# A graph-attention kernel whose order is planned: other costs in the plan, and a dot product carried in the query rows

## The chip, the cores and the metric

The kernel runs on one core of a Trainium2 chip. The metric is the device time of one execution in microseconds (us), taken as the median of several executions. TensorE is PE in the profile (its weight loads are PEld), VectorE is DVE, ScalarE is ACT, GpSimd is POOL and SyncE, which only starts DMAs here, is SP.

## The reference

There are 32 batches of 512 nodes with 512 features, in float32, and one sparse 512 x 512 adjacency matrix `adj` (about 4 edges for each node). Two layers follow each other, both on a layer norm and a relu of their input:

```
h = relu(layernorm(x))
q, k, v = h @ Wq + bq, h @ Wk + bk, h @ Wv + bv        # 8 heads of 64
out = softmax(q k' / 8, over the edges of adj) v
x = x + out @ Wo + bo                                  # layer 0
h = relu(layernorm(x)) ; hw = h @ W
s1, s2 = hw @ a1, hw @ a2
att = softmax(leaky_relu(s1_i + s2_j) * adj, over all j)
x = x + elu(att @ hw + beta * hw)                      # layer 1
```

In layer 1 a pair without an edge has the exponent 0, so each row is a sum over all nodes plus a correction over its edges.

## The kernel before

**Tiles and stages.** A batch is 4 tiles of 128 nodes (T = 4). `stage_a(b)` fetches x, normalizes it, transposes it and makes queries (`queries`), keys and values (`keys_and_values`, with seven half products for each pair of tiles). They go to tables in DRAM: `qtab` for q, `tab` for k and v. `stage_b(b)` works through edges. Each tile of 128 nodes has 4 groups of 128 edge slots. For each group POOL gathers the rows of k and v of the edge's source (`gather`, L939) and the row of q of the edge's node (L959) by indirect DMA. `layer0` multiplies q and k (L990), sums each head (L993), takes the exponent on ACT (L999), weights the rows of v (L1004), and PE sums the edges of each node into PSUM (`edge_sums`, L977). The result is divided by the sum of the weights (L1028), transposed (L734), copied out of PSUM (L1041), multiplied by Wo (L41) and added to x (L1043). Then come the norm, the relu and two dot products with rows of W a (L1051): s2 as column 0 of the row `hx`, which is stored for layer 1, and s1 of the node in a tile of its own.

Layer 1 of batch b runs with layer 0 of batch b + 2 (LAG = 2), so that one gather brings k and v of one batch and hx of the older one in a single row of `tab`. The last two batches have no such partner, and gather hx alone from `th`. `edge_weights` adds s1 of the edge's node and s2 of its source (L1109), and makes the weights `wv`; `layer1` sums hx by them, adds the column sums of the whole batch (`cs`), and ends with the product by W (L41), the elu (L1171, L1172, L1176, L1177) and the write to the output.

**s1 for each edge.** Before the change, `self_sums` does this once in a batch: PE transposes the four columns of s1 (L1080), ACT copies them out, SP writes them to DRAM as one row (L1083) and reads that row back into all 128 partitions (L1088, 256 KB, into a buffer of the ring "q"). DVE multiplies it with the one-hot matrix OH (L1092) and sums groups of 32 (L1093), which leaves s1 of each edge's node in `s1e`. `self_sums` also makes the column sums: PE sums the rows of hx (L1071), with each of the 4 sums repeated in 32 rows, ACT copies them (L1075), PE transposes them, and DVE reduces all 512 columns of the result (L1077).

**What sets the order.** Nothing is issued in the order of the source. Each step is recorded by `op` with an engine, a cost in us, a key (the time at which it is wished, in steps S of 20 us for each tile) and what it reads and writes. `Plan.order` then plays the work through: on each engine it takes, of the steps that could start first, the one with the smallest `rank`, gives it a buffer of its ring, and books its cost. The instructions are issued in the order of the planned starts, and each engine keeps to that order on the chip. Three constants matter here. `PACE` (L71) multiplies the costs of DVE and ACT. `FREE` (L69) is subtracted from the key of those DVE and ACT steps that read or write PSUM, so that they come earlier. The rings (L271 on) give the number of buffers: a step that takes a buffer can't be planned before one of its ring is free, and on the chip it waits until the last reader of that buffer, a store included, is done.

The lines of the change as the profile names them: L787 (q out of PSUM), L859 (k and v out of PSUM), L890 (stores of q, k and v by SP), L959 (gather of q), L990, L993, L1075 to L1100 (`self_sums`), L1109 (s1 + s2).

Of the kernel before, what the change touches and what calls it, by code (L numbers as in the profile page):

```python
# [9 lines left out]
F32 = mybir.dt.float32  # L10
I32 = mybir.dt.int32
AF = mybir.ActivationFunctionType
ALU = mybir.AluOpType
# [18 lines left out]
KO, VO, HO = 0, 512, 512 + 8 * VW  # L32
HW_ = 520
ROW = HO + HW_
LAG = 2
DUMMY = 4

# [26 lines left out]
class Plan:  # L64
# [1 line left out]


    STAY, WAIT = 1.0, 0.2
    FREE = 5.0  # L69

    PACE = {"DVE": 0.9, "ACT": 0.93}  # L71

    LAG = {"PE": 0.25, "DVE": 0.12, "ACT": 0.2, "POOL": 0.15, "SP": 0.0}

# [4 lines left out]
    def buf(self, tag, name=""):  # L79
        return Buf(tag, name)  # L80
# [137 lines left out]
def kernel(  # L218
# [49 lines left out]
    def ring(n, shape, name):  # L268
        return [wtile(shape, f"{name}{i}") for i in range(n)]
# [4 lines left out]
        "S": ring(3, [P, C // 2, P], "S"),  # L274
        "oT": ring(1, [P, C, P], "oT"),
        "gT": ring(1, [P, C, P], "gT"),
        "q": ring(2, [P, D], "q"),
        "k": ring(2, [P, D], "k"),
        "v": ring(5, [P, H, VW], "v"),
        "kv": ring(5, [P, 2, ROW], "kv"),  # L280
        "qe": ring(2, [P, 2, D], "qe"),
        "w": ring(4, [P, D], "w"),
        "x1": ring(4 * LAG + 1, [P, D], "x1"),
        "hx": ring(4, [P, HW_], "hx"),
# [6 lines left out]
        "st": ring(3, [P, 6], "st"),  # L291
        "rd": ring(2, [P, T, H], "rd"),
        "dn": ring(3, [P, 3, T], "dn"),
        "s1": ring(2, [P, T], "s1"),
        "cs": ring(LAG + 1, [P, C], "cs"),
        "row": [dram.tile([N], F32, name=f"row{i}", tag=f"row{i}") for i in range(2)],
        "tab": [dram.tile([N + DUMMY, ROW], F32, name=f"tab{i}", tag=f"tab{i}") for i in range(LAG + 2)],
        "tkv": [dram.tile([N + DUMMY, HO], F32, name=f"tkv{i}", tag=f"tkv{i}") for i in range(LAG)],
        "th": [dram.tile([N + DUMMY, HW_], F32, name=f"th{i}", tag=f"th{i}") for i in range(LAG)],
        "qtab": [dram.tile([N + 1, D], F32, name=f"qtab{i}", tag=f"qtab{i}") for i in range(3)],  # L300
# [27 lines left out]
    def setup():  # L328
        nc.gpsimd.iota(OH.bitcast(I32), pattern=[[1, D]], base=1, channel_multiplier=0)
        nc.gpsimd.iota(idx[:, 0, 0:1], pattern=[[1, 1]], base=0, channel_multiplier=1)  # L330
        make_identity(nc, ident)
        nc.gpsimd.memset(mhalf, -0.5)
        nc.vector.memset(rings["qe"][-1], 0.0)
        nc.vector.memset(one32, 1.0 / G)
        for b in rings["hx"]:
            nc.vector.memset(b[:, D:], 0.0)
        for b in rings["v"]:
            nc.vector.memset(b[:, :, HD:], 0.0)
        for b in [rmax, dmax, fin]:
            nc.vector.memset(b, 0.0)  # L340

    def constants():

        def load(fn, dma=4096, w=()):
            op("SP", 0.1, 20.0, fn, w=w, dma=dma)

        for dst, src in ((bk_r, bk), (bq_r, bq)):
            load(lambda dst=dst, src=src: nc.sync.dma_start(dst, bcast_rows(src, D)), P * D * 4, [C_["rows"]])
        load(lambda: nc.sync.dma_start(beta_b, bcast_rows(beta, 1)))
        zero = rings["qe"][-1].rearrange("p a b -> p (a b)")  # L350
        for tag, n in (("tkv", D), ("qtab", D), ("th", HW_), ("tab", ROW)):
# [575 lines left out]
    def stage_b(b):  # L927
# [16 lines left out]
        for t in range(T):  # L944
            kb = base(T * b + t)
            slots = [buf("kv", f"kv{b}_{t}_{i}") for i in range(2)]
            held = [{n: buf(None, n) for n in ("K", "V", "H")} for _ in range(2)]
            of = {KO: "KVH", VO: "VH", HO: "H"}
            for g in range(NG):
                for tab, c0, c1 in st[b]["tab"]:  # L950
                    op("POOL", 1.3, kb - 0.85 * S + 0.1 * g, lambda sl=slots[g // 2], g=g, t=t, tab=tab, c0=c0, c1=c1: gather(
                        sl.ap[:, g % 2, c0:c1], tab, t, g),
                       r=[tab, C_["idx"]],
                       w=[(slots[g // 2], (g % 2, c0)), *((held[g // 2][n], (g % 2, "row")) for n in of[c0])],
                       dma=P * (c1 - c0) * 4)
            if s is not None:
                qs = [buf("qe", f"qe{b}_{t}_{i}") for i in range(2)]
                for g in range(NG):
                    op("POOL", 1.3, kb - 0.84 * S + 0.1 * g, lambda q=qs[g // 2], g=g, t=t: nc.gpsimd.indirect_dma_start(  # L959
                        q.ap[:, g % 2, :], None, s["qtab"].ap,  # L960
                        bass.IndirectOffsetOnAxis(ap=qidx[:, t, g : g + 1], axis=0),
                        bounds_check=N, oob_is_err=False),
                       r=[s["qtab"], C_["qidx"]], w=[(qs[g // 2], g % 2)], dma=P * D * 4)
            wvb = edge_weights(b - LAG, t, kb, slots, held) if old is not None else None
# [17 lines left out]
    def layer0(b, t, kb, slots, held, qs, weights):  # L982

        s = st[b]
        for i in range(2):
# [1 line left out]
            sb = buf("s", "s")  # L987

            def mult(qe=qe, sl=sl):
                nc.vector.tensor_tensor(qe.ap, qe.ap, sl.ap[:, :, KO : KO + D], op=ALU.mult)  # L990

            def total(qe=qe, sb=sb):
                nc.vector.tensor_reduce(  # L993
                    sb.ap, qe.ap.rearrange("p n (h f) -> p n h f", f=HD), axis=AX.X, op=ALU.add
                )

            def expo(sl=sl, sb=sb):
# [8 lines left out]
            op("DVE", 1.24, key, mult, r=use([sl], [held[i]], "K"), w=[qe])  # L1006
            op("DVE", 1.2, key, total, r=[qe], w=[sb])
# [55 lines left out]
    def self_sums(b, key):  # L1063
# [5 lines left out]
        def col_sums():  # L1069
# [10 lines left out]
        o = op("PE", 0.15, key + 0.485 * S, lambda: nc.tensor.transpose(ps.ap[0:T, 0:P], s["s1"].ap, ident), r=[s["s1"]], w=[ps])  # L1080
        plan.reserve(o, s1t)
# [3 lines left out]
        s1b, s1e = buf("q", f"s1b{b}"), buf("s1e", f"s1e{b}")  # L1085
        s["s1e"] = s1e

        op("SP", 0.1, key, lambda: nc.sync.dma_start(s1b.ap, row.ap.unsqueeze(0).to_broadcast([P, N])),  # L1088
           r=[row], w=[s1b], dma=P * N * 4)

        def pick():
            nc.vector.tensor_tensor(s1b.ap, OH, s1b.ap, op=ALU.mult)  # L1092
            nc.vector.tensor_reduce(  # L1093
                s1e.ap.rearrange("p t g -> p (t g)"), s1b.ap.rearrange("p (s r) -> p s r", r=G), axis=AX.X, op=ALU.add
            )

        op("DVE", 1.4, key + 0.8 * S, pick, r=[C_["OH"]], w=[s1b, s1e])
        op("DVE", 0.2, key + 0.9 * S, lambda: nc.vector.scalar_tensor_tensor(
            fin, s["mv1"].ap[:, :, 0:2], 0.0, fin, op0=ALU.mult, op1=ALU.add), r=[s["mv1"]], w=[C_["fin"]])
        op("DVE", 0.2, key + 0.9 * S, lambda: nc.vector.tensor_tensor(rmax, rmax, s["rd"].ap, op=ALU.max),  # L1100
           r=[s["rd"]], w=[C_["rmax"]])

    def edge_weights(b, t, kb, slots, held):

        s = st[b]
        k1 = kb + 0.6 * S
        z, wvb = buf("z", f"z{b}_{t}"), buf("wv", f"wv{b}_{t}")
        for i in range(2):
            op("DVE", 0.2, k1, lambda i=i: nc.vector.tensor_tensor(  # L1109
                z.ap[:, 2 * i : 2 * i + 2], s["s1e"].ap[:, t, 2 * i : 2 * i + 2], slots[i].ap[:, :, HO], op=ALU.add),  # L1110
               r=[s["s1e"], *use([slots[i]], [held[i]], "H")], w=[z])
# [318 lines left out]
```

## Time and profile before

| | |
|---|---|
| median of 10 runs | 2746.71 us (2740.95 to 2752.78) |
| the profiled execution | 2743.47 us |
| its span, first to last instruction | 2741.6 us |
| granted TensorE clock, mean | 0.989 |
| DMA | 796.71 MB, mean 291 GB/s |
| DMA queue of POOL (gathers) | 643.93 MB, 69.6% of 16 engines |
| DMA queue of SP (stores, loads) | 150.15 MB, 14.9% of 16 engines |

Times are of one profiled execution. Busy time of an engine counts its instructions, and "(x53)" behind it is their number. A line of the timeline gives the start, the duration, the engine, the line of the kernel, the operation, output and input, how many records were merged, and in brackets the idle time before it and what ended that. A float32 product is two records, so "x8" is four products. The granted clock is 1.00 where TensorE ran at full speed.

Queries, keys and values are made from the first microseconds on until 2553 us, and layer 0 of the first batch reaches its edges at 99 us. So the run has a fill at its start, a long middle that repeats every 82 us (one batch), and a drain from 2553 us on.

### The profile page before, as it was taken

To read this page: it belongs to the slowest core of one execution; us is meant where nothing else is said; L and a number is where in the kernel's file an instruction comes from. 1 tells how busy PE (TensorE), PEld (TensorE's weight loads), DVE (VectorE), ACT (ScalarE), POOL (GpSimd) and SP (SyncE) were. 2 spreads that over 40 slices of the span, in tenths; PEclk is the share of its full clock that TensorE was granted. 3 is DMA by queue.
4 is the path that set the end of the run, shared out by engine and by line. 5 is a ranking of instruction groups with operands and counts; after the bars stand their busy time and mean duration, and the time that the engine had idled before them with its cause. 6 is when DMAs were issued, how large, how long until landed. Compare 5 with 4: busy or idle time off the path is not lost.

```text
span 2741.6 us, 39873 instructions
## 1 busy us (share of the span) xinstructions
PE 2661.2 (97%) x10250; PEld 1210.8 (44%) x10250; DVE 2091.0 (76%) x5138; ACT 1936.6 (71%) x6245; POOL 1823.8 (67%) x1710
## 2 busy tenths in 40 slices
PE   8999999999999999999999999999999999999886
PEld 4444444444444444444444444444444444444332
DVE  8768778777777777787877777777778777777663
ACT  1557777777777677777777777777777777777763
POOL 2866676676676676776676676666666676676663
PEclk9999999999999999999999999999999999999988
DMA  5988898888898888988888888888898898898863
GB/s 178 295 260 324 316 307 294 311 293 304 304 306 290 304 305 279 328 295 292 310 302 297 306 301 302 299 306 301 296 314 304 282 319 289 296 321 281 300 208 106
DMA packets 242019, 796.71 MB, mean 291 GB/s; under 512 B 35267, under 2 KB 35395, under 8 KB 241782
## 3 DMA queue, kind: packets, MB, share of 16 engines
q0 software_dynamic: 156736, 643.93, 69.6%
q1 hardware_dynamic: 85046, 150.15, 14.9%
q8 instruction: 83, 1.36, 0.2%
q14 instruction: 154, 1.26, 0.1%
HBM read 624.70 MB, written 169.26 MB: 290 GB/s over the span
## 4 chain that ended last, share of the span: by engine, by line
PE 87%; DVE 4%; DMA 3%; ACT 3%; issue 2%; POOL 1%; another core or an unknown queue 0%; POOLq 0%; SPq 0%; DVEq 0%; ACTq 0%
PE pd L41 44%; PE pd L851 26%; PE pd L734 6%; PE pd L977 4%; PE px L977 4%; ACT kv L1004 2%; DMA kv<-tab,idx 2%; PE pd L911 1%; DMA qe<-qtab,qidx 1%; PE pd L1071 1%; DVE s L993 1%; DVE qe L990 0%; POOL kv L939 0%; DVE w L1028 0%; DMA x<-in_x_dram,perm 0%
## 5 line engine op out<-in xcount | busy, mean ns | idle before, releaser
L1004 ACT ACTIVATE kv<-kv 128x64 f32<-128x64 f32 x4096 | 1011.5, 336 | 5.6
L959 POOL DMA_INDIRECT qe<-qtab,qidx x512 | 557.8, 1089 | 264.6 <-issue 119.6
L939 POOL DMA_INDIRECT kv<-tab,idx x480 | 516.0, 1075 | 164.9 <-issue 111.1
L41 PE MATMUL pd<-w,gT 128*128 128x512 f32 x1024 | 467.3, 599 | 5.9 <-ACT gT L1162 4.9
L41 PE MATMUL pd<-wo,oT 128*128 128x512 f32 x1032 | 469.2, 598 | 1.6 <-ACT oT L1041 1.4
L41 PE MATMUL pd<-wq,hT 128*128 128x512 f32 x1024 | 462.8, 595 | 0.0
L759 POOL DMA_INDIRECT x<-in_x_dram,perm x252 | 355.1, 1409 | 89.7 <-issue 60.8
L990 DVE TENSOR_TENSOR qe<-qe,kv 128x1024 f32<-128x1024 f32 x256 | 313.0, 1223 | 41.6 <-DMA kv<-tab,idx 25.4
L993 DVE TENSOR_REDUCE s<-qe 128x16 f32<-128x1024 f32 x256 | 311.0, 1215 | 0.7
L41 PEld LDWEIGHTS pd<-w,gT 128*128 128x128 f32 x1024 | 196.2, 192 | 252.6 <-issue 234.6
L41 PEld LDWEIGHTS pd<-wo,oT 128*128 128x128 f32 x1032 | 196.6, 192 | 245.2 <-issue 232.6
L41 PEld LDWEIGHTS pd<-wq,hT 128*128 128x128 f32 x1024 | 194.5, 191 | 244.7 <-issue 241.9
L764 POOL DMA_INDIRECT out_dram<-w,perm x128 | 149.0, 1164 | 202.4 <-DVE w L1177 142.5
L746 POOL TENSOR_TENSOR mv<-mv,mhalf 128x1 f32<-128x1 f32 x256 | 166.5, 658 | 140.4 <-DVE mv L743 104.0
L851 PE MATMUL pd<-wk,hT 128*128 128x512 f32 x496 | 240.6, 610 | 4.9 <-ACT kv L999 2.4
L851 PE MATMUL pd<-wt,S 128*128 128x512 f32 x496 | 237.9, 602 | 1.9 <-ACT v L873 1.4
L851 PE MATMUL pd<-wv,S 128*128 128x512 f32 x496 | 233.5, 593 | 0.0
L734 PE MATMUL pd<-ident,w 128*128 128x128 f32 x1152 | 160.7, 278 | 30.8 <-DVE w L1028 15.6
L1051 DVE CUSTOM_DVE_ANT_0 w<-hx,wa_r 128x512 f32<-128x512 f32 x256 | 175.9, 687 | 9.1 <-ACT hx L753 6.3
L1171 ACT ACTIVATE w<-pd,dn 128x512 f32<-128x512 f32 x128 | 86.7, 677 | 135.8 <-PE pd L41 120.5
L1043 DVE TENSOR_TENSOR x<-pd,x 128x512 f32<-128x512 f32 x128 | 88.1, 689 | 122.8 <-PE pd L41 95.8
L741 DVE BATCH_NORM_STATS2 st<-x 128x6 f32<-128x512 f32 x256 | 176.4, 689 | 5.9 <-DMA x<-in_x_dram 1.7
(201 smaller groups left out, 3557.8 us busy)
## 6 DMA issues: line engine op xcount, KB each, us to landing
qtab<-q SPq DMA_DIRECT2D x124, 256.0 KB
tab<-hx SPq DMA_DIRECT2D x120, 260.0 KB
tab<-v SPq DMA_DIRECT2D x120, 260.0 KB
tab<-k SPq DMA_DIRECT2D x120, 256.0 KB
qe<-qtab,qidx POOLq DMA_INDIRECT x512
q<-row SPq DMA_DIRECT2D x32, 256.0 KB
kv<-tab,idx POOLq DMA_INDIRECT x480
x<-in_x_dram,perm POOLq DMA_INDIRECT x252
```

The costliest lines, as they stand in the source:

```text
L41: nc.tensor.matmul(out, lhsT, rhs, start=start, stop=stop)
L734: nc.tensor.transpose(p[:, ts(c, P)], src[:, ts(c, P)], ident)
L741: nc.vector.bn_stats(s6.ap, src.ap)
L759: nc.gpsimd.indirect_dma_start(dst, None, rows, bass.IndirectOffsetOnAxis(ap=perm[:, t : t + 1], axis=0), **lim)
L851: nc.tensor.matmul(p.ap, lhs()[:, c, :], rhs[:, c, :], start=first and c == 0, stop=c == K2 - 1, skip_group_check=True)
L939: nc.gpsimd.indirect_dma_start(dst, None, tab.ap, bass.IndirectOffsetOnAxis(ap=idx[:, t, g : g + 1], axis=0), bounds_check=N + DUMMY - 1, ...
L959: op("POOL", 1.3, kb - 0.84 * S + 0.1 * g, lambda q=qs[g // 2], g=g, t=t: nc.gpsimd.indirect_dma_start(q.ap[:, g % 2, :], None, s["qtab"]. ...
L977: nc.tensor.matmul(out(g), lhs(g), slots[g // 2].ap[:, g % 2, c0 : c0 + n], start=True, stop=True)
L990: nc.vector.tensor_tensor(qe.ap, qe.ap, sl.ap[:, :, KO : KO + D], op=ALU.mult)
L993: nc.vector.tensor_reduce(sb.ap, qe.ap.rearrange("p n (h f) -> p n h f", f=HD), axis=AX.X, op=ALU.add)
L1004: nc.scalar.activation(p[:, h, 0:HD], p[:, h, 0:HD], AF.Copy, scale=p[:, h, HD : HD + 1])
L1051: nc.vector.tensor_tensor_reduce(scr.ap, hx.ap[:, 1 : D + 1], row, 1.0, 0.0, op0=ALU.mult, op1=ALU.add, accum_out=dst)
```

## The change

- In the plan, `PACE` goes from 0.9 (DVE) and 0.93 (ACT) to 1.0, and `FREE` from 5 to 10, half a step.
- A row of q gets 4 more columns (QW = 516 in place of 512), and column 512 holds s1 of the same node two batches earlier, which DVE copies there. `qtab`, its stores and the gathers of q carry it. `edge_weights` adds s1 from the gathered q row (a buffer `qe`) in place of `s1e`.
- The way of s1 over transpose, row, broadcast and pick moves into `spread_s1`, and is left for the last two batches only.
- The ring "k" has one buffer in place of two, and "s1" three in place of two.
- The column sums: ACT scales them by 32 as it copies them, and DVE reduces every 32nd column only.

```
-    FREE = 5.0
+    FREE = 10.0
-    PACE = {"DVE": 0.9, "ACT": 0.93}
+    PACE = {"DVE": 1.0, "ACT": 1.0}
...
-        "q": ring(2, [P, D], "q"),
-        "k": ring(2, [P, D], "k"),
+        "q": ring(2, [P, QW], "q"),
+        "k": ring(1, [P, D], "k"),
-        "qe": ring(2, [P, 2, D], "qe"),
+        "qe": ring(2, [P, 2, QW], "qe"),
-        "s1": ring(2, [P, T], "s1"),
+        "s1": ring(3, [P, T], "s1"),
...
-        op("DVE", 0.7, key, lambda: nc.vector.tensor_tensor(q.ap, p.ap, bq_r, op=ALU.add), r=[p, C_["rows"]], w=[q])
+        op("DVE", 0.7, key, lambda: nc.vector.tensor_tensor(q.ap[:, 0:D], p.ap, bq_r, op=ALU.add), r=[p, C_["rows"]], w=[(q, "q")])
+        if b >= LAG:
+            s1 = st[b - LAG]["s1"]
+            op("DVE", 0.1, key, lambda: nc.vector.tensor_copy(q.ap[:, D : D + 1], s1.ap[:, t : t + 1]),
+               r=[(s1, t)], w=[(q, "s1")])
...
-        op("ACT", 0.6, key, lambda: nc.scalar.copy(csr.ap, pc.ap), r=[pc], w=[csr])
+        op("ACT", 0.6, key, lambda: nc.scalar.activation(csr.ap, pc.ap, AF.Copy, scale=float(G)), r=[pc], w=[csr])
...
-        op("DVE", 0.69, key + 0.5 * S, lambda: nc.vector.tensor_reduce(
-            cs.ap, pt.ap.rearrange("p (c q) -> p c q", c=C), axis=AX.X, op=ALU.add), r=[pt], w=[cs])
+        op("DVE", 0.2, key + 0.5 * S, lambda: nc.vector.tensor_reduce(
+            cs.ap, pt.ap[:, 0 :: G].rearrange("p (c q) -> p c q", c=C), axis=AX.X, op=ALU.add), r=[pt], w=[cs])
+        if b + LAG >= B:
+            spread_s1(b, key)
...
+            def add(i=i):
+                s1 = s["s1e"].ap[:, t, 2 * i : 2 * i + 2] if qs is None else qs[i].ap[:, :, D]
+                nc.vector.tensor_tensor(z.ap[:, 2 * i : 2 * i + 2], s1, slots[i].ap[:, :, HO], op=ALU.add)
```

More of the change, by code (lines that the diff above doesn't have):

```diff
@@ L34 @@
 ROW = HO + HW_
+QW = 516
 LAG = 2
@@ L299 @@
         "th": [dram.tile([N + DUMMY, HW_], F32, name=f"th{i}", tag=f"th{i}") for i in range(LAG)],
-        "qtab": [dram.tile([N + 1, D], F32, name=f"qtab{i}", tag=f"qtab{i}") for i in range(3)],
+        "qtab": [dram.tile([N + 1, QW], F32, name=f"qtab{i}", tag=f"qtab{i}") for i in range(3)],
         "D": [psum.tile([P, D], F32, name=f"pd{i}", tag=f"pd{i}") for i in range(6)],
@@ L336, in setup @@
             nc.vector.memset(b[:, D:], 0.0)
+        for b in rings["q"]:
+            nc.vector.memset(b[:, D:], 0.0)
         for b in rings["v"]:
@@ L350, in constants @@
         zero = rings["qe"][-1].rearrange("p a b -> p (a b)")
-        for tag, n in (("tkv", D), ("qtab", D), ("th", HW_), ("tab", ROW)):
+        for tag, n in (("tkv", D), ("qtab", QW), ("th", HW_), ("tab", ROW)):
             for tab in rings[tag]:
@@ L957, in stage_b @@
                 qs = [buf("qe", f"qe{b}_{t}_{i}") for i in range(2)]
+                for q in qs:
+                    q.q, q.s1 = buf(None, "q"), buf(None, "s1")
                 for g in range(NG):
@@ L962, in stage_b @@
                         bounds_check=N, oob_is_err=False),
-                       r=[s["qtab"], C_["qidx"]], w=[(qs[g // 2], g % 2)], dma=P * D * 4)
-            wvb = edge_weights(b - LAG, t, kb, slots, held) if old is not None else None
+                       r=[s["qtab"], C_["qidx"]], w=[(x, g % 2) for x in (qs[g // 2], qs[g // 2].q, qs[g // 2].s1)],
+                       dma=P * QW * 4)
+            wvb = edge_weights(b - LAG, t, kb, slots, held, qs if s is not None else None) if old is not None else None
             pv = layer0(b, t, kb, slots, held, qs, old is not None) if s is not None else None
@@ L989, in mult @@
             def mult(qe=qe, sl=sl):
-                nc.vector.tensor_tensor(qe.ap, qe.ap, sl.ap[:, :, KO : KO + D], op=ALU.mult)
+                nc.vector.tensor_tensor(qe.ap[:, :, 0:D], qe.ap[:, :, 0:D], sl.ap[:, :, KO : KO + D], op=ALU.mult)
             def total(qe=qe, sb=sb):
                 nc.vector.tensor_reduce(
-                    sb.ap, qe.ap.rearrange("p n (h f) -> p n h f", f=HD), axis=AX.X, op=ALU.add
+                    sb.ap, qe.ap[:, :, 0:D].rearrange("p n (h f) -> p n h f", f=HD), axis=AX.X, op=ALU.add
                 )
@@ L1004, in weigh @@
                     nc.scalar.activation(p[:, h, 0:HD], p[:, h, 0:HD], AF.Copy, scale=p[:, h, HD : HD + 1])
-            op("DVE", 1.24, key, mult, r=use([sl], [held[i]], "K"), w=[qe])
-            op("DVE", 1.2, key, total, r=[qe], w=[sb])
+            op("DVE", 1.24, key, mult, r=[(qe, "use"), *use([sl], [held[i]], "K")], w=[qe.q])
+            op("DVE", 1.2, key, total, r=[(qe, "use"), qe.q], w=[sb])
             op("ACT", 0.25, key, expo, r=[sb, (sl, "use")], w=[held[i]["V"]])
@@ L1074, in self_sums, with spread_s1 @@
         plan.reserve(o, csr)
-        op("ACT", 0.6, key, lambda: nc.scalar.copy(csr.ap, pc.ap), r=[pc], w=[csr])
+        op("ACT", 0.6, key, lambda: nc.scalar.activation(csr.ap, pc.ap, AF.Copy, scale=float(G)), r=[pc], w=[csr])
         op("PE", 0.45, key + 0.49 * S, lambda: turned(pt.ap, csr.ap), r=[csr], w=[pt])
-        op("DVE", 0.69, key + 0.5 * S, lambda: nc.vector.tensor_reduce(
-            cs.ap, pt.ap.rearrange("p (c q) -> p c q", c=C), axis=AX.X, op=ALU.add), r=[pt], w=[cs])
+        op("DVE", 0.2, key + 0.5 * S, lambda: nc.vector.tensor_reduce(
+            cs.ap, pt.ap[:, 0 :: G].rearrange("p (c q) -> p c q", c=C), axis=AX.X, op=ALU.add), r=[pt], w=[cs])
+        if b + LAG >= B:
+            spread_s1(b, key)
+        op("DVE", 0.2, key + 0.9 * S, lambda: nc.vector.scalar_tensor_tensor(
+            fin, s["mv1"].ap[:, :, 0:2], 0.0, fin, op0=ALU.mult, op1=ALU.add), r=[s["mv1"]], w=[C_["fin"]])
+        op("DVE", 0.2, key + 0.9 * S, lambda: nc.vector.tensor_tensor(rmax, rmax, s["rd"].ap, op=ALU.max),
+           r=[s["rd"]], w=[C_["rmax"]])
+    def spread_s1(b, key):
+        s = st[b]
         ps, s1t, row = buf("D", "ps1"), buf("wv", f"s1t{b}"), buf("row", f"row{b}")
@@ L1086, in self_sums, with edge_weights @@
         s["s1e"] = s1e
-        op("SP", 0.1, key, lambda: nc.sync.dma_start(s1b.ap, row.ap.unsqueeze(0).to_broadcast([P, N])),
+        op("SP", 0.1, key, lambda: nc.sync.dma_start(s1b.ap[:, 0:N], row.ap.unsqueeze(0).to_broadcast([P, N])),
            r=[row], w=[s1b], dma=P * N * 4)
         def pick():
-            nc.vector.tensor_tensor(s1b.ap, OH, s1b.ap, op=ALU.mult)
+            nc.vector.tensor_tensor(s1b.ap[:, 0:N], OH, s1b.ap[:, 0:N], op=ALU.mult)
             nc.vector.tensor_reduce(
-                s1e.ap.rearrange("p t g -> p (t g)"), s1b.ap.rearrange("p (s r) -> p s r", r=G), axis=AX.X, op=ALU.add
+                s1e.ap.rearrange("p t g -> p (t g)"), s1b.ap[:, 0:N].rearrange("p (s r) -> p s r", r=G), axis=AX.X, op=ALU.add
             )
         op("DVE", 1.4, key + 0.8 * S, pick, r=[C_["OH"]], w=[s1b, s1e])
[L1098 to L1103, printed above, removed]
+    def edge_weights(b, t, kb, slots, held, qs):
         s = st[b]
@@ L1108, in edge_weights @@
         for i in range(2):
-            op("DVE", 0.2, k1, lambda i=i: nc.vector.tensor_tensor(
-                z.ap[:, 2 * i : 2 * i + 2], s["s1e"].ap[:, t, 2 * i : 2 * i + 2], slots[i].ap[:, :, HO], op=ALU.add),
-               r=[s["s1e"], *use([slots[i]], [held[i]], "H")], w=[z])
+            def add(i=i):
+                s1 = s["s1e"].ap[:, t, 2 * i : 2 * i + 2] if qs is None else qs[i].ap[:, :, D]
+                nc.vector.tensor_tensor(z.ap[:, 2 * i : 2 * i + 2], s1, slots[i].ap[:, :, HO], op=ALU.add)
+            op("DVE", 0.2, k1, add, r=[*([s["s1e"]] if qs is None else [(qs[i], "use"), qs[i].s1]),
+                                       *use([slots[i]], [held[i]], "H")], w=[z])
         op("DVE", 0.2, k1, lambda: nc.vector.scalar_tensor_tensor(
```

## The prediction

> **What bounds the kernel now.** I read the page's busy table first, then the busy time by stretch, then PE's waits, then PE's timeline around the longest gaps.
>
> ```profile
> span 2741.6 us, 39873 instructions
> PE 2661.2 (97%) x10250; PEld 1210.8 (44%) x10250; DVE 2091.0 (76%) x5138; ACT 1936.6 (71%) x6245; POOL 1823.8 (67%) x1710
> ```
>
> PE is busy for 97% of the span and every other engine has a fifth or more to spare. So only two things shorten this run: less work on PE, and less of the 80.4 us (2741.6 - 2661.2) in which PE stands still. Where it stands still, by stretch (length, PE, PEld, DVE, ACT, POOL busy, granted clock, DMA share, GB/s):
>
> ```profile
> 100.00:160.00 60.00, 52.30 (x173) 23.08 (x166) 37.18 (x73) 33.35 (x117) 49.04 (x45) 0.92 0.99 306
> 160.00:300.00 140.00, 137.64 (x529) 61.79 (x529) 111.72 (x248) 97.70 (x328) 92.29 (x90) 1.00 0.86 301
> 300.00:2555.00 2255.00, 2242.03 (x8725) 1022.22 (x8727) 1758.37 (x4295) 1671.17 (x5415) 1535.82 (x1432) 1.00 0.87 301
> 2555.00:2660.00 105.00, 82.21 (x342) 35.85 (x335) 69.45 (x183) 75.04 (x247) 71.11 (x64) 0.89 0.81 260
> 2660.00:2742.00 82.00, 56.32 (x200) 23.05 (x198) 32.31 (x108) 28.55 (x68) 32.44 (x32) 0.87 0.37 111
> ```
>
> There are three kinds of time. The fill loses 7.7 us from 100 to 160 and 2.4 us up to 300. The middle loses only 13.0 us in 2255. The drain, in which no queries, keys or values are left to fill PE with, loses 22.8 + 25.7 = 48.5 us. Most of the rest goes before 20 us. Who ends PE's waits in the middle:
>
> ```profile
> PE pd L734 <- DVE w L1028: 7.0, 9, 2.4
> PE pd L851 <- ACT v L875: 1.4, 2, 1.3
> PE pd L851 <- ACT v L873: 1.4, 4, 0.7
> PE pd L851 <- ACT hT L779: 1.0, 3, 0.4
> PE pd L851 <- ACT pd L1172: 0.8, 1, 0.8
> ```
>
> Seven of the 13 us are one place: the transposes of the attention output wait for the division (L1028) that reads PSUM. The rest are ACT's readers of PSUM. PE's timeline shows the gaps in fill and middle, and one more thing:
>
> ```profile
> 104.72 0.66 PE L734 MATMUL pd<-ident,w 128*128 128x128 f32 x4 [2.26 <-DVE rd L1032]
> 156.42 5.40 PE L851 MATMUL pd<-wk,hT 128*128 128x512 f32 x8 [2.40 <-ACT kv L999]
> 964.60 0.66 PE L734 MATMUL pd<-ident,w 128*128 128x128 f32 x4 [2.36 <-DVE w L1028]
> ```
>
> ```profile
> 955.00:970.00 15.00, 12.64 (x58) 6.14 (x57) 12.77 (x29) 13.21 (x45) 12.00 (x10) 0.89 0.65 181
> ```
>
> The last line is the stretch around 964 us, its columns as above. Eight records of 512 columns step 3.44 us elsewhere and take 5.40 behind the gap of 2.40. The gap of 2.36 lies in a stretch with a granted clock of 0.89, so 0.11 x 15 = 1.65 us of clock are lost with it. A gap of over 2 us thus costs itself and some 1.7 us more: I count 4 us for each.
>
> On this the Trainium skill, "TensorE: Matmul & The Clock Gate", section "HAM oscillation - how this bites in real kernels", says that only gaps above about 3.4 us throttle PE. This trace shows it at 2.36 us, so the row decides. By the page's rule the middle would have no clock loss at all, and the sum below would be the same.
>
> **The change part by part.**
>
> *s1 in the q row, PE.* 30 of the 32 transposes of s1 go (L1080; those of the last two batches stay). PE's timeline puts the next transpose 0.11 us behind the s1 transpose, so 0.11 us each is what PE gets back:
>
> ```profile
> 2557.36 0.27 PE L1080 MATMUL pd<-ident,s 128*4 128x128 f32 x1
> 2557.47 0.60 PE L734 MATMUL pd<-ident,w 128*128 128x128 f32 x4
> ```
>
> 30 x 0.11 = **-3.3 us**, on the path.
>
> *s1 in the q row, other engines.* DVE loses 30 picks (L1092 and L1093, 0.686 each: -41 us). It loses 32 x (0.687 - 0.2) = -16 us in the reduction of the column sums, which reads 16 elements in place of 512 (nearest row: L1032, 128x8, 0.204). It gains 120 one-column copies, at the 0.153 of L743: +18. Net -39 us of 2091. ACT loses 30 x 0.25. SP loses 60 issues, and the queues 30 x 256 KB. All this lies beside a PE that is 99% busy in the middle: 0 on the path. The product L990 reads rows of pitch 516; between no change and +5% (0.06 x 256 = 15 us of DVE) I take none, as the element count stays.
>
> *Wider rows.* 512 gathers carry 128 x 16 B more, +1.05 MB against -7.9 MB for the broadcasts. In the trace's packet records the median packet of 4,096 bytes of the GpSimd queue (two rows of 2,048) took 159 ns, and one of 4,160 (two rows of 2,080) 161 ns. So 2,064-byte rows cost about 1%. Bounds: -1 us (one broadcast less in the drain) to +2 us; I take 0. The Trainium skill, "DMA: Bandwidth & Descriptors", section "How a descriptor splits into AXI transactions", speaks against this edit: a row that is no multiple of 256 B needs a left-over transaction, and one that starts unaligned more. As an estimate that page would make the q gathers 2 to 12% dearer; the 161 ns for rows of 2,080, which are as uneven, do not show the 12%.
>
> *The new waits.* The copy of s1 writes into q, so in DVE's queue it waits for the store of the q tile two before; q tiles are about 20 us apart, so that is 40 us old. It also needs s1 of batch b-2, which the keys place 0.7 to 1.1 steps of 20 us earlier. Behind it in DVE's order stand the next normalisation and the addition for q. The edge weights read s1 from the gathered q row; DVE's order places that addition beside the product on the same tile, so no slot is held longer. **One k buffer for two**: the first addition of a k tile now waits for the landing of the previous tile's store. In the new DVE order the work between them is at least 9 us by the rows, 11.7 us at DVE's share of 0.79. The nearest store that the chain times, th<-hx, landed 6.27 us after its issue. Covered by 5 us; 0.
>
> *The new order, middle.* From the thirteenth batch on PE repeats one sequence per batch, as before. Before: column sums, s1, four transposes of the attention output. Now: column sums, four transposes of x (0.44 us), then those of the attention output. The nine waits on L1028 get 0.33 us more cover: 8 x 0.33 + 0.2 = -2.8. The waits on ACT's PSUM readers come to 4.6; these readers now rank half a step earlier, and I take half of it, -2.3. Together **-5 us**; bounds 0 and -14.7 (all 13.0 idle plus 1.7 of clock), with a loss possible only as in the third rival.
>
> *The new order, fill and drain.* The fill loses 10.1 us idle and 3 x 1.7 of clock. The order there is quite another one: batches 4 to 8 mix queries and layer 1 irregularly, and pull work from later batches ahead. Bounds -12 (nearly all of it gone) to +20 (five more gaps of 4 us); I take 0, since no row shows it. In the drain PE's sequence is almost the same and its chain is gathers, weighting and single dense products; -5 to +6, I take 0.
>
> **Sum**: -3.3 - 5 = -8.3 us. The profiled execution took 2743.5 us (span 2741.6), so 2735.2. It lies 3.2 us under the median of 2746.7, so I forecast a median of **2738 us**.
>
> **The rivals.**
> 1. *The fill gains too.* With the middle as above and two of its three long gaps gone (8 us) the median is 2730. For it: PSUM readers that rank higher would end the waits of 104 and 142 us earlier. Against: DMA is at 0.99 there.
> 2. *Nothing to gain but the s1 work.* The middle's waits stay or move, as PE is already 99.4% busy in it: 2746.7 - 3.3 = 2743. For it: DVE and ACT lose work that nobody waited for.
> 3. *The fill gets new gaps (slower).* Place: batches 3 to 8, 160 to 650 us, where the new order has not settled and the q stores wait for layer 0 two batches earlier. Price: 4 us a gap. With 8.3 us won elsewhere, it is slower by more than 0.2% from four gaps on (16 - 8.3 = 7.7); with five it is 2746.7 + 20 - 8.3 = 2758. Against: the planner's costs of DVE and ACT are now above the step of the rows (0.7 for 0.60), so real engines run ahead of its order.
>
> **How the numbers follow.** Forecast 45%, rival 1 10%, rival 2 25%, rival 3 20%. A measurement here can tell about 0.2%, 5.5 us, from no change, so forecast and rival 1 count as faster (55%), rival 2 as same (25%), rival 3 as slower (20%). The forecast's own range is 2732 to 2741. The range for 8 in 10 runs from 2724 (all the middle's 14.7 plus 3.3 plus 5 of the fill) to 2755 (rival 3 with four gaps).
>
> **What would show it.** The s1 transposes counted at 2; DVE busy near 2050; the middle's PE idle near 8 us; the waits on L1028 below 5 us in the middle; the fill's loss between 100 and 300 unchanged near 10 us and the drain's near 48. Wrong, if k's first addition waits for its store (then the single buffer is the bound), if q gathers last visibly longer, or if gaps above 2 us stand between 160 and 650 us.

## The result, and the profile after

The changed kernel took 2732.45 us (median of 9 runs, 2725.62 to 2737.86), the kernel before 2746.51 beside it: a ratio of 0.9946, with a 95% interval of 0.9937 to 0.9955. In a second timing the ratio was 0.9944 (0.9923 to 0.9966). The forecast was 2738 us, with faster as the likeliest sign.

The busy table of the changed kernel, then its busy time by stretch (length, PE, PEld, DVE, ACT, POOL busy, granted clock, DMA share, GB/s). The drain is read 15 us earlier than before, as it begins earlier.

```profile
span 2727.0 us, 39762 instructions
PE 2648.9 (97%) x10220; PEld 1213.8 (45%) x10220; DVE 2050.9 (75%) x5200; ACT 1939.7 (71%) x6215; POOL 1817.1 (67%) x1710
```

```profile
100.00:160.00 60.00, 54.18 (x180) 23.78 (x179) 39.21 (x79) 32.95 (x111) 46.59 (x42) 0.94 0.98 262
160.00:300.00 140.00, 133.74 (x511) 60.06 (x510) 103.65 (x239) 97.42 (x331) 92.88 (x90) 0.98 0.83 294
300.00:2540.00 2240.00, 2229.04 (x8679) 1022.79 (x8678) 1722.70 (x4355) 1669.74 (x5369) 1530.11 (x1432) 1.00 0.87 301
2540.00:2645.00 105.00, 84.15 (x380) 39.29 (x379) 75.74 (x202) 80.95 (x268) 70.52 (x64) 0.93 0.81 274
2645.00:2727.00 82.00, 57.24 (x204) 23.17 (x202) 32.03 (x106) 28.93 (x69) 36.72 (x36) 0.91 0.43 127
```

By this table hardly anything has happened: PE's idle time from 300 to 2540 us went from 13.0 (2240 - 2227.03 in the kernel before) to 11.0. What changed is where it stands. From 1100 to 2100 us, the kernel before and then the changed one:

```profile
1100.00:2100.00 1000.00, 995.76 (x3881) 457.05 (x3880) 785.98 (x1921) 744.85 (x2406) 684.04 (x641) 1.00 0.88 304
1100.00:2100.00 1000.00, 1000.00 (x3884) 459.52 (x3883) 774.15 (x1952) 748.46 (x2410) 687.62 (x643) 1.00 0.87 303
```

All but 0.7 us of the 11.0 lie ahead of 900 us. PE's waits from 300 to 2540 us, in which the division (now L1038) had 7.0 us in nine pieces before:

```profile
PE pd L737 <- DVE w L1038: 3.2, 3, 1.9
PE pd L858 <- ACT hT L782: 2.5, 2, 1.9
PE pd L858 <- DVE v L866: 1.9, 1, 1.9
PE pd L987 <- DVE wv L1140: 1.6, 1, 1.6
```

Idle time can't say what a batch costs, so I read it from PE's timeline: the column sums run once in a batch, and the time from one batch's to the next is the **period**. Before, it wanders between 80.95 and 85.4 from batch 8 to batch 28, with a mean of 81.9. Afterwards it is 80.95 to 80.99 in every batch from 10 to 28. The same marks cut the run into three parts. These are the marks of batch 8 and batch 28, before (L1071) and after (L1081):

```profile
836.85 1.05 PE L1071 MATMUL pd<-hx,one 128*32 128x512 f32 x8
2474.37 1.04 PE L1071 MATMUL pd<-hx,one 128*32 128x512 f32 x8
848.87 1.04 PE L1081 MATMUL pd<-hx,one 128*32 128x512 f32 x8
2470.35 1.05 PE L1081 MATMUL pd<-hx,one 128*32 128x512 f32 x8
```

"Mark 8" is when batch 8 reaches its column sums, "8 to 28" the twenty batches behind it, and "rest" what is left of the span. Each line is one profiled execution; the last column is the median of the kernel before, timed beside it, and kernels that share one value of it ran together on one chip.

| kernel | span | mark 8 | 8 to 28 | rest | before there |
|---|---|---|---|---|---|
| before | 2741.6 | 836.9 | 1637.5 | 267.2 | 2746.5 |
| after | 2727.0 | 848.9 | 1621.5 | 256.7 | 2746.5 |
| before, again | 2741.8 | 840.3 | 1638.3 | 263.2 | 2746.8 |
| after, again | 2734.6 | 852.1 | 1620.5 | 262.0 | 2746.8 |
| `o_spread` | 2738.8 | 837.1 | 1638.2 | 263.5 | 2746.8 |
| `a_k2` | 2746.6 | 840.8 | 1639.9 | 265.9 | 2746.8 |
| `b_plan` | 2724.9 | 836.5 | 1620.6 | 267.9 | 2733.7 |
| `a_oldplan` | 2715.8 | 832.5 | 1618.2 | 265.1 | 2733.7 |
| `a_free5` | 2731.9 | 836.7 | 1621.4 | 273.8 | 2733.7 |
| `a_pace09` | 2734.5 | 850.1 | 1622.4 | 262.0 | 2733.7 |
| `mix2340` | 2727.4 | 832.7 | 1620.3 | 274.4 | 2735.8 |
| `a_dummy` | 2732.8 | 847.9 | 1625.4 | 259.5 | 2735.8 |
| `a_spread` | 2735.8 | 848.4 | 1621.5 | 265.9 | 2735.8 |
| `a_hw516` | 2735.2 | 842.4 | 1628.4 | 264.4 | 2735.8 |

The change wins 16.0 us in the middle (17.8 the second time) and arrives there 12.0 us later (11.8). The rest is 10.6 shorter in the first pair and 1.1 in the second; the kernel before alone differs by 4.0 from one profile to the other there, the changed one by 5.3. So the middle is the one gain that both pairs show in full.

What PE waited for in these twenty batches of the kernel before is more than one thing. The listed idle time of the first profile is 10.7 us, of which 7.0 end with the division; in the second it is 10.7 again, of which 5.5 do. Most of the rest ends with ACT's readers of PSUM. In the changed kernel 1.9 and 0.8 us are left of all of it, and none of that ends with the division. A tile of the kernel before that waits looks like this, on PE and on DVE:

```profile
1900.25 1.06 PE L977 MATMUL px<-kv,OH 128*32 128x260 f32 x16
1902.96 0.27 PE L1080 MATMUL pd<-ident,s 128*4 128x128 f32 x1
1903.90 0.66 PE L734 MATMUL pd<-ident,w 128*128 128x128 f32 x4 [0.67 <-DVE w L1028]
```

```profile
1902.71 0.21 DVE L1032 RECIPROCAL rd<-px 128x8 f32<-128x8 f32 x1 [1.02 <-PE pd L911]
1903.16 0.68 DVE L1028 TENSOR_TENSOR w<-px,rd 128x512 f32<-128x512 f32 x1
```

The sums of the tile end at 1901.31. The reciprocal starts 1.40 us later and the division ends at 1903.84, so PE has nothing to do between the s1 transpose and the transposes of the divided output.

The late fill is seen in PE's timeline of the changed kernel:

```profile
146.34 3.78 PE L858 MATMUL pd<-wt,S 128*128 128x512 f32 x4 [3.74 <-DVE k L866]
165.04 3.43 PE L858 MATMUL pd<-wv,S 128*128 128x512 f32 x4 [1.86 <-DVE S L847]
223.60 1.11 PE L737 MATMUL pd<-ident,w 128*128 128x128 f32 x4 [2.84 <-DVE w L1038]
```

Four records of 512 columns take 1.88 elsewhere, and 3.78 and 3.43 behind these gaps. In the longest of them PE waits for an addition of k, which stands in DVE's queue behind a step that waits for POOL:

```profile
144.50 0.16 DVE L751 SCALAR_TENSOR_TENSOR mv<-mv 128x1 f32<-128x1 f32 x1 [2.87 <-POOL mv L749]
```

By the granted clock the fill loses 10.2 us, where it lost 5.1 before. Some 6.8 of them are behind these three gaps. The other 3.4 are lost from 49 to 56 us, where PE has no gap at all (the last section has the rows).

### The profile page after: what moved, and what is told of

Same layout as the page of the kernel before. It is cut to its first block, busy times and chain, and to the rows that moved or that the text cites. A ratio compares the mean times of both kernels' runs of the same rounds, so it can differ in the third digit from the quotient of the medians.

```text
span 2727.0 us, 39762 instructions
## 1 busy us (share of the span) xinstructions
PE 2648.9 (97%) x10220; PEld 1213.8 (45%) x10220; DVE 2050.9 (75%) x5200; ACT 1939.7 (71%) x6215; POOL 1817.1 (67%) x1710
## 4 chain that ended last, share of the span: by engine, by line
PE 90%; DVE 3%; issue 3%; DMA 2%; POOL 1%; ACT 1%; another core or an unknown queue 0%; SPq 0%; POOLq 0%; DVEq 0%; ACTq 0%
PE pd L42 47%; PE pd L858 26%; PE pd L737 7%; PE pd L987 4%; PE px L987 4%; DMA qe<-qtab,qidx 1%; PE pd L918 1%; PE pd L1081 1%; POOL kv L946 0%; POOL qe L968 0%; ACT kv L1014 0%; DVE qe L1000 0%; DMA kv<-tab,idx 0%; POOL x L762 0%
## 5 line engine op out<-in xcount | busy, mean ns | idle before, releaser
L968 POOL DMA_INDIRECT qe<-qtab,qidx x512 | 549.4, 1073 | 233.3 <-issue 117.6
L1000 DVE TENSOR_TENSOR qe<-qe,kv 128x1024 f32<-128x1024 f32 x256 | 312.5, 1222 | 41.8 <-DMA qe<-qtab,qidx 27.8
L767 POOL DMA_INDIRECT out_dram<-w,perm x128 | 157.2, 1228 | 148.6 <-DVE w L1196 103.4
L737 PEld LDWEIGHTS pd<-ident,w 128*128 128x128 f32 x1152 | 134.4, 143 | 93.4 <-issue 41.7
```

The costliest lines, as they stand in the source:

```text
L737: nc.tensor.transpose(p[:, ts(c, P)], src[:, ts(c, P)], ident)
L1000: nc.vector.tensor_tensor(qe.ap[:, :, 0:D], qe.ap[:, :, 0:D], sl.ap[:, :, KO : KO + D], op=ALU.mult)
```

## The experiments

**1. Which part does it?** Four kernels on one chip, on which the kernel before took 2733.65 (26 runs). `b_plan` is the kernel before with the constants alone:

```
-    FREE = 5.0
+    FREE = 10.0
-    PACE = {"DVE": 0.9, "ACT": 0.93}
+    PACE = {"DVE": 1.0, "ACT": 1.0}
```

> The kernel before with the two constants of the plan alone (PACE 1.0, FREE 10), s1 still over transpose, row, broadcast and pick, two k buffers. Theory P (the plan's constants end the middle's waits, s1 only its 3.3 us): 14.1 - 3.3 = 10.8 us less than before, 2735.7; the middle's period falls from 81.7 to 81.0. Theory S (the s1 column does it, the plan nothing): 2746.5.

Measured: 2727.31 us, 0.9974 (0.9964 to 0.9984).

`a_oldplan` is the changed kernel with both constants set back, so the column, the rings and the column sums alone:

```
-    FREE = 10.0
+    FREE = 5.0
-    PACE = {"DVE": 1.0, "ACT": 1.0}
+    PACE = {"DVE": 0.9, "ACT": 0.93}
```

> The changed kernel with the old constants (PACE 0.9 and 0.93, FREE 5): the s1 column, one k buffer and the shorter column sums alone. Theory P: 3.3 us less than before, 2743.2, period still 81.6. Theory S: 2732.5, period 81.0.

Measured: 2719.58 us, 0.9945 (0.9927 to 0.9964).

`a_free5` sets only `FREE` back to 5, and `a_pace09` only `PACE` to 0.9 and 0.93.

> The changed kernel with FREE back at 5 and PACE at 1.0. If full durations do it (they give each planned wait some slack): as the change, 2732.5. If the earlier PSUM readers do it: near 2743, with waits of PE on ACT's readers of PSUM back.

Measured: 2734.52 us, 1.0000 (0.9990 to 1.0010).

> The changed kernel with PACE back at 0.9 and 0.93 and FREE at 10. If full durations do it: near 2743, with PE waiting for the division again in the middle (about 0.25 us a batch). If the earlier PSUM readers do it: 2732.5.

Measured: 2730.88 us, 0.9989 (0.9978 to 0.9999).

That the constants do it (theory P) falls: the column alone gives as much as the whole change gave elsewhere, and adding one constant to it takes most or all of it away. That they do nothing (theory S) falls too, as `b_plan` is 6.3 us faster with them alone. The table says where. All four have a short middle, 1618 to 1622; the kernel before was not profiled on this chip, so what its middle takes here isn't known. With the column, `FREE` = 10 makes the fill late (848.9 and 850.1) and `FREE` = 5 doesn't (832.5 and 836.7), and with `FREE` = 5 and `PACE` = 1.0 the rest is the longer one (273.8).

**2. Is it the work that the column removes?** `before` and `after` were run once more for their parts (the table's lines "again"):

> The kernel before, profiled once more, beside the variants. If the stalls of its middle belong to its order of work, the 20 batches between the marks of batch 8 and batch 28 take again about 1637 us (16 more than the changed kernel's 1621), with periods between 80.95 and 82.3. If they belong to the one execution profiled first, they take 1618 to 1625, and the middle is no source of the gain.

> The changed kernel, timed once more beside the others. Ratio to the kernel before 0.993 to 0.996 (the first result: 0.9946). If its late fill belongs to its order of work, the mark of batch 8 is at 846 to 851 us again; if to one execution, it is near 837, where the kernel before has it.

Measured: middle 1638.3 and 1620.5, mark 8 of the changed kernel 852.1 (846 to 851 was expected), ratio 0.9944. Both the stalls of the middle before and the late fill after belong to the kernels, not to one execution.

`o_spread` is `a_oldplan` (the column with the old constants) and does the old work for s1 in every batch as well. It leaves no part of the computation out; only the last two batches use the results.

```
-        if b + LAG >= B:
-            spread_s1(b, key)
+        spread_s1(b, key)
```

> The version with the column in the q rows and the planner constants of before, but the old way of s1 (transpose, row in DRAM, broadcast, pick) is done for every batch as well; its results are used by the last two batches only. Without the additional work this version took 0.9945 of the kernel before. Theory W (what the column removes is worth the time itself): the ratio goes back to 0.998 to 1.000, and the period in the middle rises from 80.91 to 81.3 or more. Theory O (PE pays at most 0.1 us for a transpose, and the rest of the old way lies beside PE; the gain is that the order changed): the period stays within 80.9 to 81.05, and the ratio is 0.993 to 0.997, but for what the order of fill and drain moves.

Measured: 2745.28 us, 0.9993 (0.9981 to 1.0004), with a period of 82.0: the numbers of theory W. By this run alone the removed work would be worth the whole gain. But the addition also gave another order, and most of the loss stands in one place of that order. PE's timeline of `o_spread`:

```profile
1183.34 1.06 PE L987 MATMUL px<-kv,OH 128*32 128x260 f32 x16
1184.33 1.98 PE L858 MATMUL pd<-wt,S 128*128 128x512 f32 x4
1186.68 0.66 PE L737 MATMUL pd<-ident,w 128*128 128x128 f32 x4 [0.37 <-DVE w L1038]
```

The sums of a tile end at 1184.4, and only one half product stands between them and the transposes of the divided output. DVE's timeline has the division there:

```profile
1185.48 0.21 DVE L1042 RECIPROCAL rd<-px 128x8 f32<-128x8 f32 x1 [0.71 <-PE px L987]
1185.61 0.11 DVE L1161 TENSOR_SCALAR dn<-px 128x1 f32<-128x1 f32 x1
1185.75 0.17 DVE L1162 RECIPROCAL dn<-dn 128x1 f32<-128x1 f32 x1
1185.83 0.20 DVE L1163 TENSOR_SCALAR dn<-dn,beta_b 128x1 f32<-128x1 f32 x1
1185.94 0.68 DVE L1038 TENSOR_TENSOR w<-px,rd 128x512 f32<-128x512 f32 x1
```

From the start of the reciprocal to the end of the division it is 1.14 us (1185.48 to 1186.62), and PE starts 0.06 later. So a tile needs 1.1 us of other work on PE between its sums and its transposes (I call this work its **cover**), and as much more as the reciprocal starts behind the end of the sums, here another 1.08 us. In 36 of the 49 tiles from 1100 to 2100 us of `o_spread` the transposes follow the division within 0.06 us, which I read as PE waiting for it, or being just in time.

The sum over PE's timeline agrees. Counted from the start of one PE instruction to the next, a period of `o_spread` (batches 18 to 26) takes 1.09 us more than one of `a_oldplan`. The half products `pd<-wt,S`, which stand before these transposes, take 0.68 of it, the transposes of `w`, which come in more and smaller groups there, 0.35, and the s1 transpose 0.11.

`a_spread` makes the same addition to the changed kernel with its own constants, so the old work is there and the order is another one.

> The changed kernel, constants included, with the old way of s1 done for every batch as well. In the version with the old constants the same addition gave back the whole gain (0.9993); there its order left 1.7, 1.7, 1.3 and 1.7 us of PE's work between the sums of a tile and the transposes of its divided output. Here the order repeats only from the eighteenth batch on, and leaves 2.3, 8.6, 3.0 and 6.9 us, as the changed kernel does (2.2, 8.6, 3.0, 6.9). Theory C (that cover decides the middle): from the eighteenth batch on the period is 81.0 to 81.15, the transpose included, though DVE, SP and the queues carry the old load. Theory W (the old work itself costs): the period is 81.6 or more there too. The fill is another order again, so the total is open: 0.993 to 1.000.

Measured: 2733.97 us, 0.9989 (0.9980 to 0.9999). From the eighteenth batch on its period is 80.95 to 80.97, and from 1700 us on PE stands still in none of it:

```profile
1700.00:2400.00 700.00, 700.00 (x2757) 323.05 (x2748) 549.07 (x1383) 520.92 (x1684) 464.76 (x451) 1.00 0.88 304
```

This is the changed kernel's period, with all the old transposes, picks and broadcasts in it. Theory W falls, and theory C holds between these two kernels: **the order of work decides the middle, by the cover that it leaves, and the removed work costs the period next to nothing.** They ran on different chips. But from the start of the reciprocal to the end of the division it is 1.13 to 1.14 us on both, and the changed kernel has its 80.96 on the chip of `o_spread` too (`after, again`), so the chip doesn't explain the 82.0.

How much cover the orders leave for the four tiles of a batch, and what the middle does with it, from the batch on from which the order repeats (batch 10 for the kernel before):

| kernel | cover, us | least time from division to transposes | period |
|---|---|---|---|
| before | 1.8, 8.6, 3.0, 6.9 | 0.06, most often 0.4 for the first tile | 80.95 to 82.3 |
| `o_spread` | 1.7, 1.7, 1.3, 1.7 | 0.06 | 82.0 |
| `a_oldplan` | 1.7, 5.2, 3.0, 1.7 | 0.4 | 80.91 |
| after | 2.2, 8.6, 3.0, 6.9 | 0.9 | 80.96 |
| `a_spread` | 2.3, 8.6, 3.0, 6.9 | 0.9 from batch 18 on | 80.96 |
| `b_plan` | 4.0, 8.6, 3.0, 6.9 | 1.8 | 81.03 |

The kernel before has the covers of the changed one, less 0.4 for the first tile, but its reciprocal starts anything from 0.1 to 4.0 us behind the sums; in the changed kernel each tile has its own delay (0.1, 0.5 to 1.0, 0.6, 0.8 to 1.2). `a_oldplan` shows that 1.7 us do, where the reciprocal starts 0.1 us behind. So cover alone doesn't rank the kernels; it is the cover less the delay that does. In the kernel before, 12 of the 80 tiles of these twenty batches wait for the division. What sets the delay there I didn't test, and no run separates these waits from those for ACT's readers, which went as well.

**3. What a transpose costs PE.** `a_dummy` is the changed kernel with one more transpose, overwritten, ahead of each batch's column sums; the planner doesn't know of it, so every engine has the order of the changed kernel.

```
         def col_sums():
+            nc.tensor.transpose(pc.ap[0:T, 0:P], s["hx"][T - 1].ap[:, 1 : T + 1], ident)
             for t in range(T):
```

> The changed kernel with one more transpose (4 columns of hx) ahead of the column sums of each batch, its result overwritten: 32 instructions of the form that the change took from PE, and the order on every engine otherwise the same. The forecast's price is 0.11 us each: the period rises from 80.96 to 81.07, and the time by 3.5 us, a ratio 0.0013 above that of the changed kernel (0.9944 to 0.9946), so 0.995 to 0.997. If a transpose fits into a pause that PE has anyway, the period stays at 80.96. If what it costs is the reload of the stationary matrix, the period rises by 0.2 or more.

Measured: 2734.73 us, 0.9993 (0.9984 to 1.0002), above the range expected, which was reckoned from the ratio of the changed kernel on another chip; its period is 81.25, 0.29 above. This is also what was expected if the load of its stationary matrix were the price (0.2 or more). PE's timeline points at its place instead. PE's timeline of `a_dummy`:

```profile
1172.18 1.04 PE L918 MATMUL pd<-v,one 128*32 128x512 f32 x8
1173.15 0.27 PE L1080 MATMUL pd<-ident,hx 128*4 128x128 f32 x1
1173.35 1.07 PE L1082 MATMUL pd<-hx,one 128*32 128x512 f32 x8
1174.35 0.66 PE L737 MATMUL pd<-ident,x 128*128 128x128 f32 x4
```

From 512 columns to 128 and back, the steps are 0.97 and 0.20 where the changed kernel goes from L918 to the column sums in one step of 0.86: 0.31 more. The real s1 transpose, which loads a matrix of the same size (128*4), stood next to other transposes. In `a_spread`, with it:

```profile
2065.09 1.04 PE L1081 MATMUL pd<-hx,one 128*32 128x512 f32 x8
2066.06 0.27 PE L1099 MATMUL pd<-ident,s 128*4 128x128 f32 x1
2066.17 0.60 PE L737 MATMUL pd<-ident,x 128*128 128x128 f32 x4
2066.61 1.47 PE L737 MATMUL pd<-ident,w 128*128 128x128 f32 x12
```

and in the changed kernel, without:

```profile
1174.90 1.04 PE L1081 MATMUL pd<-hx,one 128*32 128x512 f32 x8
1175.87 0.66 PE L737 MATMUL pd<-ident,x 128*128 128x128 f32 x4
1176.37 1.47 PE L737 MATMUL pd<-ident,w 128*128 128x128 f32 x12
```

From the column sums to the last group it is 1.52 with it and 1.47 without. Its own price is 0.05 us, as the first group behind the column sums pays 0.06 more whoever it is. So the load is not what makes `a_dummy` dear.

**4. What makes the fill late?** `a_k2` gives k two buffers again; hx rows get 516 columns in place of 520 to make room. `a_hw516` is its control: those rows, and one k buffer.

```
-HW_ = 520
+HW_ = 516
-        "k": ring(1, [P, D], "k"),
+        "k": ring(2, [P, D], "k"),
```

> The changed kernel with two buffers for k, as before; hx rows have 516 columns in place of 520, to make room. Theory K (the single k buffer makes the fill late: PE waits 3.74 us on k at 146 us): the mark of batch 8 comes at 836 to 840 us in place of 848.9, and the ratio is 0.989 to 0.992. Theory R (the fill is late because of the order that the constants give, and the wait on k is a part that another wait replaces): the wait on k is gone, the mark of batch 8 stays at 844 us or later, and the ratio is 0.993 to 0.997.

Measured: 2753.89 us, 1.0031 (1.0014 to 1.0048). The fill is as early as in the kernel before on that chip (840.8 and 840.3), but the middle is lost: its order never repeats, and its periods run from 79 to 86.

> The changed kernel with hx rows of 516 columns in place of 520, and its single k buffer: the control of the version with two k buffers, which has the same rows and took 1.0031. The planner books transfers by their size, so this edit alone gives another order, one that repeats only from batch 22 on. Theory K (the second k buffer is what unsettles the middle): ratio 0.993 to 0.996, with the late fill of the changed kernel. Theory R (any other order of fill and middle, whatever the reason, moves the time by 10 us or more): mark of batch 8 and periods before batch 22 differ from the changed kernel's 848.9 to 852.1 and 80.96, with periods of 81.5 to 85 where the covers are 0.9 to 1.7 us, ratio 0.997 to 1.004.

Measured: 2734.58 us, 0.9991 (0.9982 to 1.0000). Four columns that nobody reads move mark 8 to 842.4, and the periods ahead of batch 22, where the order begins to repeat, to between 79 and 86 (80.9 behind it). So theory R holds, and `a_k2` doesn't tell what the second buffer does: much of what it moved, an edit without meaning moves too. The clean pair for the fill is in the first experiment: `a_pace09` differs from `a_oldplan` by `FREE` alone, ran on the same chip, and its mark 8 comes 17.6 us later. The changed kernel and `a_free5`, which also differ by `FREE` alone, are 12.2 us apart, though they were not timed together.

**5. The parts put together.** `mix2340` uses the old constants for steps wished before 2340 us and the new ones behind that.

```
+    LATE = 2340.0
...
+        late = key >= self.LATE
+        o = Op(eng, us * (1.0 if late else self.PACE.get(eng, 1.0)), key, fn, r, w, [], dma)
...
+        o.rank = key - (10.0 if late else self.FREE) * evict
```

> The changed kernel with the planner's old constants for everything wished before 2340 us (keys), and the new ones behind it: the order of fill and middle of the version with the column alone (its mark of batch 8 came at 832.5 us, its period is 80.91), and in the drain the order of the changed kernel. If the three stretches add up, as they do if each belongs to its own order: mark of batch 8 at 830 to 838 us, period 80.9 to 81.0, ratio 0.990 to 0.994, below both kernels. If the drain of the changed kernel was short only in one execution (177.8 us, then 183.6 in the second), the ratio is 0.993 to 0.996, that of the column alone.

Measured: 2732.45 us, 0.9991 (0.9981 to 1.0000). The fill and the middle are those of `a_oldplan` to 2 us, but the rest takes 274.4, the longest of all. So the parts don't add up. That the last tiles depend on what fill and middle have left over is my guess; no run shows it. The fastest of these kernels is `a_oldplan`; it and the changed kernel were not timed together, so which of the two is faster isn't measured.

## Why the forecast was right, and where not

- **Sign and size.** 14.1 us were won by the medians, 8.3 were summed. That the two lie so near each other is partly luck: the middle gave three times its term, and the late fill, whose term was 0, took 12 of that back. The offset from profile to median was right (3.2 assumed, 3.6 measured: 2732.45 and 2728.83).
- **s1 transposes, -3.3.** Too large: 30 x 0.05 = 1.5 us. Two of 32 are left, as said. The 0.11 was the step to the next instruction, but 0.06 of it falls on whichever transpose comes first.
- **Other engines' s1 work, 0.** Right: DVE fell to 2050.9 (2050 said), and `a_spread` pays nothing in its period for having the work back.
- **Wider rows, 0.** Right: packets of 4,128 bytes (two rows of 2,064) took 160 ns in the median, and the product L1000 on the wider rows 1222 ns, where it took 1223. On the descriptor split, which as the forecast said speaks against this edit, the Trainium skill ("DMA: Bandwidth & Descriptors", "How a descriptor splits into AXI transactions") names left-over transactions, from which the forecast estimated 2 to 12%; that is not borne out here, as 160 against 159 ns is under 1%.
- **One k buffer, 0.** Right in its own terms: in the first 860 us of the changed kernel DVE's k additions wait for PE, never for a store. The 3.74 us in which PE waits for k come from DVE's queue, where a step that waits 2.87 us for POOL stands ahead of it.
- **Order in the middle, -5 (0 to -14.7).** Both kinds of wait that the forecast named, for the division and for ACT's readers of PSUM, did go, and in the twenty batches not in part but wholly. So the size failed: 16.0 us in the marks, of which 1 is the transposes, and 17.8. The forecast's four transposes of x do add 0.4 to the first tile's cover (1.8 to 2.2). The bound was wrong because it was PE's listed idle time. In `o_spread` a period has 1.07 us too much, 9.1 in 700 us, of which the profile lists 3.2 as idle; the rest lies in steps that it books as busy. In the fence above, the half product at 1184.33 has a step of 2.35, about 0.5 more than the 1.82 of the same form behind the sums in the changed kernel, and 0.37 of it is listed.
- **Fill, 0 (-12 to +20).** Wrong sign, inside its bounds: +12, as in the third rival, though not by its count. Only one gap above 2 us lies between 160 and 650 us in the first profile (two in the second), and one more at 142 us; the clock pays for them and for the gap of 1.86. And 3.4 us of clock go from 49 to 56 us without any gap, which no term of the forecast had.
- **Drain, 0 (-5 to +6).** -10.6 and -1.1 in the two pairs: not settled, as two executions of one kernel differ by up to 5.3 there. Fill and rest together come to 1104 and 1104 us before and to 1106 and 1114 after: the gain is that of the middle.

What stays open: why `FREE` = 10 makes the fill late, tile by tile; what delays the reciprocal in the kernel before; and what the change is worth on the chips where the kernel before takes 2734 to 2736 us, as the changed kernel itself was not run there. The kernel before is 11 to 13 us shorter on those chips, and if that lies in its middle, less of the middle is left to gain there.

## What to carry to other kernels

Where a planner decides the order, even an edit of four unused columns can give another one, worth 6 to 10 us here in the fill and 7 in the middle; compare a part's effect only between kernels with the same order, or name the row that the order moves. Measure a stage that repeats by its period, not by its idle time, and look for the chain that a PE instruction waits on: here 1.1 us of DVE work behind the sums of a tile, and an order that puts enough other work beside it. An order that repeats isn't yet a good one: `o_spread` repeats too, at 82.0 us.

## What the runs showed of the hardware

The clock also halves behind gaps below 2 us, but not always. The forecast knew of 2.36; in the changed kernel a gap of 1.86 us at 163 us is followed by a granted clock of 0.83 over ten microseconds, and one of 1.89 at 642 us by 1.00. PE's timeline at the second gap, and the busy time of the two stretches:

```profile
643.77 0.66 PE L737 MATMUL pd<-ident,w 128*128 128x128 f32 x4 [1.89 <-DVE w L1038]
644.26 1.88 PE L858 MATMUL pd<-wk,hT 128*128 128x512 f32 x4
```

```profile
160.00:170.00 10.00, 8.14 (x33) 3.51 (x32) 7.96 (x19) 4.03 (x12) 7.37 (x8) 0.83 1.02 394
640.00:650.00 10.00, 8.11 (x45) 4.43 (x38) 7.08 (x20) 7.88 (x27) 7.86 (x8) 1.00 0.91 278
```

So no length of gap near 2 us separates the two. The Trainium skill, "TensorE: Matmul & The Clock Gate", section "HAM oscillation — how this bites in real kernels", puts the limit at about 3.4 us; both of these gaps are shorter, and one of them paid.

The clock also halves where no gap is listed. In the changed kernel PE is busy for all of the 7.00 us from 49 to 56 us, and the granted clock there is 0.53. Ahead of it stand 32 records of only 18 columns:

```profile
46.34 4.08 PE L42 MATMUL pd<-kv,kv 128*128 128x18 f32 x32
50.25 6.63 PE L42 MATMUL pd<-wq,hT 128*128 128x512 f32 x8
```

```profile
49.00:56.00 7.00, 7.00 (x16) 3.75 (x16) 0.77 (x6) 0.00 (x0) 3.05 (x3) 0.53 0.39 126
```

Eight records of 512 columns take 3.60 elsewhere and 6.63 here. The second profile of the changed kernel has the same drop at 50 us; the kernel before has the same 32 records from 42.9 us on and keeps its full clock. What decides between the two isn't shown.

The kernel before took 2746.8 us on one chip (2746.5 in the first timing) and 2733.65 and 2735.76 on two others, up to 0.5% apart at unchanged code. No profile of it was taken on these two, so where the 11 to 13 us lie isn't known. So ratios from different chips can't be set side by side to this accuracy.
